# Softmax sums as 32x32 matmul tiles in one stretch per step, in a two-layer lookup convolution

## The chip, the cores and the metric

The kernel runs on one core of a Trainium2 chip. The metric is the device time in microseconds, from the first to the last instruction of one execution. The core has a matrix engine (PE, with the loading of its stationary operand listed as PEld), a vector engine (DVE), a scalar engine (ACT), GpSimd (POOL) and a sync engine (SP) that issues most of the DMAs. Each engine works through its own instructions in program order and waits on semaphores for the others.

## The reference

The input x is 16 images of 256 channels of 28x28, in float32. Each image is normalized by groups of 8 channels, sent through the block below, and added to x.

```python
def amm_conv3x3(x, centroids, w_sub):            # centroids: C=256, k=16, s=9
    p = ...                                      # 3x3 patches of each channel: B, N=784, C, 9
    d = sum(p * p) - 2.0 * einsum('bncs,cks->bnck', p, centroids) + sum(centroids ** 2)
    attn = softmax(-d, axis=-1)                  # over the 16 codes of each channel
    lut = einsum('cks,cso->cko', centroids, w_sub)
    return einsum('bnck,cko->bno', attn, lut)

out = relu(bn1(amm_conv3x3(gn(x), centroids1, wsub1)))
out = bn2(amm_conv3x3(out, centroids2, wsub2))
out = out * sigmoid(relu(mean(out) @ w1 + b1) @ w2 + b2)
result = x + relu(out + gn(x))
```

So for each pixel and each channel there are 16 logits, one from each code, a softmax over the 16, and a sum over 256 channels and 16 codes into 256 outputs. This is done twice.

## The kernel before

The kernel never forms the table `lut`. Where the exponentials e of a channel's 16 logits are there, the nine taps of its softmax-weighted code are nine numerators (e times the codes) over one denominator (the sum of e). The numerators over the denominator, times `w_sub`, summed over channels and taps, are the output.

**Blocks and steps.** The work is cut into 128 blocks. A block is one layer, one image, one half of the 784 pixels (392 of them) and one half of the 256 channels. Each image and layer has four blocks (`BLOCKS`), and the kernel goes through them in order. A block takes two steps, so that there are some 256 steps in all. What is done in a step belongs to several blocks at once: the logits of one, the sums of the one before, the products of blocks before that.

**The order.** Nothing is scheduled by a tool. `at(step, place, function, ...)` puts a call into a table, the table is sorted by step and place, and the calls are made in that order. Every engine gets its instructions in this order and runs them as a queue.

**The matmuls of a step**, all in float32, each recorded as two passes over the array:

- `logits` (line 613, tile `lg`): patches times codes. One call is 16 matmuls of 32 rows by 32 columns, one for each of the 16 sub-arrays that the 128x128 array can be split into. There are four calls (mm = 0 to 3) for each block, two in a step. `exps` (line 624, ACT) reads each result out of PSUM and writes e, 820 ns for a half of it.
- `num_b` (line 678, tile `nb`): the denominators and the ninth numerator of a block. It is 32 matmuls of 64 rows by 32 columns, so that eight sub-arrays are used at once, in every second step.
- `num_a` (line 664, tile `na`): the other eight numerators, 32 matmuls of 64 rows by 32 columns, in the steps between.
- `product` (line 748, tile `acc`): numerators over denominators times weights, 128x128, up to nine matmuls in a step and 63 in eight steps. The 63 come from a scheme that saves products with sums and differences of the four blocks (`PRODUCTS`); the differences are made by `mix` on POOL (lines 755 and 757).

The order on PE in a step is `lg`, then `na` or `nb`, then `lg`, then `acc`.

**From sums to quotients.** `split_r` (line 688, ACT) and `join_r` (line 692, DVE) take the denominators out of `nb`, `recip_dve` (line 706) inverts them, `spread` (line 721) copies them to the rows of the numerators, and each numerator is then either scaled by DVE straight out of PSUM (`scale_a`, line 740) or copied by ACT (`copy_a`, line 734) and scaled by POOL (`scale_q`, line 729). The results lie in the tiles `qp` (pairs) and `qo` (ones), from which `product` reads.

**PSUM** is four buffers of two banks each. Every matmul result above takes one of them, by a fixed table (`ROLES`, and `EARLY` for the first steps).

In layer 2 and the first half of the channels (`wide`), one of the four e tiles of a block is not exponentiated at once, but copied, turned, reduced by its maximum and exponentiated later (`wide_copy` to `wide_exp`).

Of the kernel before, what the change touches and what calls it, by code (L numbers as in the profile page):

```python
# [8 lines left out]
F32 = mybir.dt.float32  # L9
# [8 lines left out]
P = 128  # L18
# [21 lines left out]
NQ = {"pair": 12, "one": 4}  # L40
KO = (2, 3, 4, 5, 6, 7, 8, 0, 1)
SLOT_MM = (1, 0, 2, 3)
BLOCKS = ((0, 0), (0, 1), (1, 1), (1, 0))
# [18 lines left out]
ORDER = (4, 0, 1, 2, 3)  # L62
QUEUE = (None, None, (-0.9, 0.0), (-0.4, 0.0), (0, 1.5), (1, 1.5), (4, 0.35), (5, 1.5))
# [19 lines left out]
def rows_of(m, c, a):  # L83
    r, c4, mm = c >> 1, 2 * (c & 1) + a, m & 3
    return r, c4, mm, 16 * r + 4 * mm + c4, 16 * (1 - r) + 4 * mm + c4
# [3 lines left out]
def kernel(  # L89
# [83 lines left out]
    epool = ctx.enter_context(tc.tile_pool(name="epool", bufs=7))  # L173
# [116 lines left out]
    m_cw = kst[:, 3:7]  # L290
# [42 lines left out]
    def small_bank(name, step, tag=None):  # L333
        return bank(name, step, step and ROLES["small"][step % 2], EARLY["small"].get(step) if tag is None else tag)
# [323 lines left out]
    def num_a(u, mm):  # L658
        slot, tags = SLOT_MM.index(mm), fixed(u, "na")
        bs = banks("na", after(u, 2), ROLES["na"][slot], tags and tags[slot])  # L660
        es = u["e", mm]
        for i in range(4):
            for r in range(2):
                nc.tensor.matmul(  # L664
                    bs[32 * i : 32 * i + 32, r, :N],
                    lhsT=wts["cwa", u["hh"]][64 * r : 64 * r + 64, mm, i, :],
                    rhs=es[64 * r : 64 * r + 64, i, :],
                    start=True, stop=True,
                )
        u["na", mm] = bs  # L670
# [37 lines left out]
    def mask_of(k):  # L708
        if k == 8:
            return [(xx + 16) % 32 for xx in range(32)]  # L710
        mm, r = divmod(k, 2)
        return [16 * (1 - r) + 4 * mm + (xx >> 3) for xx in range(32)]
# [22 lines left out]

    def scale_a(u, mm):
# [7 lines left out]
    def product(key, us, w, ks, first=True, last=True, step=None, cols=(0, N), tag=None):  # L744
        if first and key not in accs:
            accs[key] = bank("acc", step, step and ROLES["acc"][step % 2], EARLY["acc"].get(step) if tag is None else tag)
# [105 lines left out]
    def rank_score(o):  # L852
        nc.vector.tensor_reduce(score[:, o : o + 1], hpads[o], axis=AX.X, op=ALU.max)
        nc.vector.tensor_scalar_mul(score[:, o : o + 1], score[:, o : o + 1], posn[:, o : o + 1])
        wide = small.tile([P, 32], F32, name="score_w")
# [130 lines left out]
    def prep_cwa():  # L986
# [3 lines left out]
        for c in range(4):  # L990
            nc.vector.tensor_scalar(f[:, :, 8 * c : 8 * c + 8], src[:, :, 0:8], m_cw[:, c : c + 1], None, op0=ALU.mult)
# [234 lines left out]

    def wide_next(j):
# [8 lines left out]
    for j, u in enumerate(blocks):  # L1236
        gi, g = 8 * (j // 4), 2 * j
        for mm in range(5):
            kind = "one" if mm == 4 else "pair"
            t = g + 1 + (j > 2) if mm == 4 else g + 2 + (j > 1)  # L1240
            homes.append(((t, 1.0), 1, j, mm, kind))
            homes.append(((gi + LAST[u["r"]][0], LAST[u["r"]][1] + 0.01 * ORDER[mm]), 0, j, mm, kind))
# [6 lines left out]

    for j, u in enumerate(blocks):  # L1250
        g = 2 * j
        u["w"] = j
        wide = u["l"] == 1 and u["hh"] == 0
        for p in range(2):
# [6 lines left out]
            for q in range(2):  # L1261
                mm = 2 * p + q
                cl, sub = TURN.get((j, mm), (g + p, 0.1 + (0.2 * q if j < 3 else q)))
                at(cl, sub, logits, u, mm)
                if wide and mm == 0:
                    at(g, 0.12, wide_copy, u, mm)
                    at(g, 0.9, wide_turn, u, mm)
                    at(g, 1.38, wide_max, u, mm)
                    at(g, 1.39, wide_sub, u, mm)
                    at(g + 1, 1.22, wide_back, u, mm)  # L1270
                    at(g + 1, 1.89, wide_exp, u, mm)
                else:
                    at(cl, 1.06 if (cl, sub) == (4, 1.035) else sub + 0.01, exps, u, mm)
# [8 lines left out]
        g = 2 * j + 2 + (j > 1)  # L1282
        for i, mm in enumerate(SLOT_MM):
            at(g, 1.0 + 0.01 * i, num_a, u, mm)
# [440 lines left out]
```

## Time and profile before

| | |
|---|---|
| time, median of 2 runs | 2605.55 us (2605.37 to 2605.73) |
| the profiled execution, first to last instruction | 2606.2 us |
| mean granted clock of PE | 0.999 |
| busy share PE / DVE / ACT / POOL | 99% / 68% / 53% / 73% |

The profile is of one execution. A busy time is the time in which an engine has at least one instruction under way, so that a PE with one sub-array at work is as busy as one with sixteen. The mean duration of one matmul pass (some 0.5 us) is from its start until its result has landed; passes overlap, and what a group costs is read from when the next group starts. The tile of a matmul, such as 64*32, gives rows by columns of the array that it takes.

### The profile page before, as it was taken

How to read it: one execution, taken by the hardware profiler on the slowest of the kernel's cores; microseconds unless marked ns; L12 is line 12 of the kernel's file. 1: busy time of each engine (PE TensorE's matmuls, PEld its weight loads, DVE VectorE, ACT ScalarE, POOL GpSimd, SP SyncE). 2: the span in 40 equal slices, each digit the busy share in tenths (PEclk: the TensorE clock that was granted, in tenths of full speed). 3: DMA queues.
4: the chain of work that ended last, by engine and by line, in shares of the span. 5: the costliest groups of instructions: out<-in, count | busy, mean ns of one | idle time of the engine just before them, and what ended most of it. 6: DMA issues, size and time to landing. Idle time of an engine off the chain costs nothing.

```text
span 2606.2 us, 85832 instructions
## 1 busy us (share of the span) xinstructions
PE 2591.2 (99%) x37026; PEld 1273.2 (49%) x37026; DVE 1776.6 (68%) x3797; ACT 1371.7 (53%) x1913; POOL 1905.6 (73%) x1341
## 2 busy tenths in 40 slices
PE   8999999999999999999999999999999999999999
PEld 4444455444454444544444444444444444444445
DVE  8766656666657666566676767766776667767676
ACT  6444444444444445444445555555555655555565
POOL 6687666776567776667666887878878787787786
PEclk9999999999999999999999999999999999999999
DMA  7556656565545575564664444444344444444442
GB/s 228 166 131 184 195 166 187 160 168 170 163 141 147 157 194 173 165 172 134 176 169 103 109 112 127 119 119 120 101 126 128 118 116 112 115 124 128 117 104 66
DMA packets 213288, 372.07 MB, mean 143 GB/s; under 512 B 29496, under 2 KB 183528, under 8 KB 212328
## 3 DMA queue, kind: packets, MB, share of 16 engines
q1 hardware_dynamic: 206584, 333.75, 47.6%
q0 software_dynamic: 6176, 32.66, 3.5%
q8 instruction: 295, 4.83, 0.8%
q14 instruction: 89, 0.73, 0.1%
q10 hardware_dynamic: 144, 0.10, 0.0%
HBM read 288.46 MB, written 77.95 MB: 141 GB/s over the span
## 4 chain that ended last, share of the span: by engine, by line
PE 99%; ACT 0%; POOL 0%; DVE 0%; issue 0%; DMA 0%; POOLq 0%; ACTq 0%
PE acc L748 52%; PE lg L613 17%; PE na L664 14%; PE nb L678 14%; ACT e L624 0%; PE sep L1049 0%; POOL qp L757 0%; PE sep L1041 0%; DMA xt<-in_x 0%; PE tap L392 0%; PE sqp L374 0%; PE sqp L343 0%; POOL qp L729 0%; PE gnp L534 0%; PE gnp L551 0%
## 5 line engine op out<-in xcount | busy, mean ns | idle before, releaser
L748 PE MATMUL acc<-qp,wall 128*128 128x392 f32 (+1 forms) x3088 | 1097.5, 498 | 0.3 <-POOL qp L757 0.2
L624 ACT ACTIVATE e<-lg 128x784 f32<-128x784 f32 x960 | 737.8, 820 | 635.2 <-PE lg L613 632.0
L757 POOL TENSOR_TENSOR qp<-qp,qp 128x784 f32<-128x784 f32 x512 | 943.7, 1867 | 152.0 <-DVE qp L740 151.6
L748 PEld LDWEIGHTS acc<-qp,wall 128*128 128x128 f32 x3088 | 567.4, 190 | 504.8 <-issue 53.6
L721 DVE STREAM_SHUFFLE rb<-r 128x392 f32<-128x392 f32 x1024 | 551.5, 606 | 0.0
L613 PE MATMUL lg<-pt,wd 32*32 32x392 f32 x15872 | 469.0, 499 | 0.2
L692 DVE SCALAR_TENSOR_TENSOR r<-nb,kst,r 128x392 f32<-128x392 f32 x128 | 80.1, 626 | 447.6 <-ACT r L688 447.6
L664 PE MATMUL na<-e,cwa 64*32 64x392 f32 x8192 | 376.5, 493 | 0.0
L740 DVE TENSOR_TENSOR qp<-na,rb 128x784 f32<-128x784 f32 x352 | 334.0, 972 | 62.2 <-PE na L664 50.3
L678 PE MATMUL nb<-e,cwb 64*32 64x392 f32 x8192 | 375.2, 492 | 0.1
L729 POOL TENSOR_TENSOR qo<-qo,rb 128x392 f32<-128x392 f32 x128 | 132.5, 1035 | 297.0 <-DVE rb L717 296.2
L706 DVE RECIPROCAL r<-r 128x392 f32<-128x392 f32 x128 | 333.2, 2603 | 4.4
L729 POOL TENSOR_TENSOR qp<-qp,rb 128x784 f32<-128x784 f32 x160 | 295.7, 1858 | 2.9
L678 PEld LDWEIGHTS nb<-e,cwb 64*32 64x32 f32 x8192 | 191.5, 106 | 174.7 <-issue 24.5
L664 PEld LDWEIGHTS na<-e,cwa 64*32 64x32 f32 x8192 | 183.8, 106 | 184.0 <-issue 74.8
L613 PEld LDWEIGHTS lg<-pt,wd 32*32 32x32 f32 x15872 | 116.4, 103 | 266.6 <-issue 238.3
L748 PE MATMUL acc<-qp,w_A 128*128 128x392 f32 x512 | 182.4, 499 | 0.0
L688 ACT ACTIVATE r<-nb,kst 128x392 f32<-128x392 f32 x128 | 86.7, 678 | 165.5 <-PE nb L678 162.3
L648 POOL TENSOR_TENSOR z<-z,mx 128x1568 f32<-128x1568 f32 x32 | 91.8, 2869 | 94.8 <-DVE mx L642 94.8
L748 PE MATMUL acc<-qo,wall 128*128 128x392 f32 (+1 forms) x386 | 157.9, 491 | 0.0
L734 ACT COPY qp<-na 128x784 f32<-128x784 f32 x160 | 130.0, 813 | 23.6 <-PE na L664 22.1
L748 PEld LDWEIGHTS acc<-qp,w_A 128*128 128x128 f32 x512 | 94.6, 190 | 82.5 <-DVE qp L740 19.8
(241 smaller groups left out, 1706.4 us busy)
## 6 DMA issues: line engine op xcount, KB each, us to landing
pt<-home SPq DMA_DIRECT2D x744, 209.0 KB
pt<-home SPq DMA_DIRECT2D x744, 104.5 KB
home<-xpad SPq DMA_DIRECT2D x30, 899.0 KB
xt<-in_x SPq DMA_DIRECT2D x30, 784.0 KB
out_dram<-y SPq DMA_DIRECT2D x31, 392.0 KB
pt<-in_p SPq DMA_DIRECT2D x6, 784.0 KB
d_wS<-st SPq DMA_DIRECT2D x12, 192.0 KB
wall<-d_wS SPq DMA_DIRECT2D x4, 576.0 KB
```

What stands on the lines that cost most here:

```text
L613: nc.tensor.matmul(bk[32 * c : 32 * c + 32, :N].rearrange("p (r w) -> p r w", w=W), lhsT=(wx[u["hh"]] if early(u) else wts["wd", u["hh"]]) ...
L624: nc.scalar.activation(eg[:, 2 * i : 2 * i + 2, :], bk[:, :, :N], AF.Exp, scale=2.0)
L648: nc.gpsimd.tensor_tensor(zk, zk, mx.unsqueeze(2).to_broadcast([P, N // 4, K]), ALU.subtract)
L664: nc.tensor.matmul(bs[32 * i : 32 * i + 32, r, :N], lhsT=wts["cwa", u["hh"]][64 * r : 64 * r + 64, mm, i, :], rhs=es[64 * r : 64 * r + 64, ...
L678: nc.tensor.matmul(bs[32 * i : 32 * i + 32, r, :N], lhsT=wts["cwb", u["hh"]][64 * r : 64 * r + 64, mm, i, :], rhs=es[64 * r : 64 * r + 64, ...
L706: nc.vector.reciprocal(u["r"], u["r"])
L721: nc.vector.stream_shuffle(rb[:, r, :], u["r"], mask_of(2 * mm + r))
L729: nc.gpsimd.tensor_tensor(q, q, u.pop(("rb", mm)), ALU.mult)
L734: nc.scalar.copy(pair(u, mm), u.pop(("na", mm))[:, :, :N])
L740: nc.vector.tensor_mul(pair(u, mm), u.pop(("na", mm))[:, :, :N], rb)
L748: nc.tensor.matmul(accs[key][:, : cols[1] - cols[0]], lhsT=wl[w][:, k, :], rhs=us["q", k][:, cols[0] : cols[1]], start=first and n == 0, s ...
L757: nc.gpsimd.tensor_tensor(pair(out_u, mm), pair(in0, mm), pair(in1, mm), ALU.subtract)
```

## The change

Three things are changed together.

- `num_a` and `num_b` are cut into matmuls of 32x32 like `logits`. For the same sums this takes twice as many matmuls, each on half the rows: 64 for `na` and 64 for `nb` in place of 32 and 32.
- In the steps 10 to 251 the matmuls of `lg`, `na` and `nb` stand in one stretch (`stage_of`), and the products behind it. The stretch has six slots. A slot is two units of eight matmuls, the one on row tiles 0 and 2, the other on row tiles 1 and 3 (the two lanes). Together a slot takes all 16 sub-arrays. One lane does a logits unit, four units of denominators and a logits unit (`SUM_LANE`, "anmopb"), the other two units of numerators, two of logits, two of numerators (`TAP_LANE`, "xyabzw"). The lanes are swapped from step to step. PSUM buffers come from `LANE_TAGS`.
- For all images but the first and the last, what works on the products of an image comes a step later (`later`, `late`); products, mixes and scales are put into new orders (`KO_LANE`, `MIX_LANE`, `ORDER_LANE`). There are 14 tiles `qp` in place of 12, and 8 of e in place of 7. Two of the four numerator tiles of a block are scaled by DVE from PSUM and two are copied and scaled by POOL; one of the copies moves to DVE (`copy_dve`) outside the wide blocks. Weights and row positions are laid out to fit (`rows_of`, `mask_of`, `prep_cwa`).

```diff
+LANE_STEPS = range(10, 252)
+LANE_TAGS = (
+    {"aS": 1, "x": 2, "n": 0, "aT": 3, "bT": 1, "z": 2, "bS": 3, "acc": 1},
+    {"aS": 3, "x": 2, "n": 0, "aT": 1, "bT": 3, "z": 2, "bS": 1, "acc": 3},
+)
+SUM_LANE, TAP_LANE = "anmopb", "xyabzw"
+SUM_ORDER = (1, 2, 3, 0)
...
-    def num_a(u, mm):
...
-        for i in range(4):
-            for r in range(2):
+    def num_a(u, m2):
+        tags = fixed(u, "na")
+        for slot in (2 * m2, 2 * m2 + 1):
+            u["na", SLOT_MM[slot]] = banks("na", after(u, 2), ROLES["na"][slot], tags and tags[slot])
+        for h in range(2):
+            for lane in range(2):
+                lane_na(u, 2 * m2 + lane, h)
+
+    def lane_na(u, x, h):
+        mm, lane = 2 * (x >> 1) + h, x & 1
+        for row in (lane, lane + 2):
+            for i in range(4):
                 nc.tensor.matmul(
-                    bs[32 * i : 32 * i + 32, r, :N],
-                    lhsT=wts["cwa", u["hh"]][64 * r : 64 * r + 64, mm, i, :],
-                    rhs=es[64 * r : 64 * r + 64, i, :],
+                    u["na", x][32 * i : 32 * i + 32, row >> 1, :N],
+                    lhsT=wts["cwa", u["hh"]][32 * row : 32 * row + 32, mm, i, :],
+                    rhs=u["e", mm][32 * row : 32 * row + 32, i, :],
+                    start=(h == 0), stop=(h == 1),
+                )
+
+    def lane_nb(u, mm, lane, first, last):
+        for row in (lane, lane + 2):
+            for i in range(4):
+                nc.tensor.matmul(
+                    u["nb"][32 * i : 32 * i + 32, row >> 1, :N],
+                    lhsT=wts["cwb", u["hh"]][32 * row : 32 * row + 32, mm, i, :],
+                    rhs=u["e", mm][32 * row : 32 * row + 32, i, :],
+                    start=first, stop=last,
+                )
+
+    def lane_lg(u, mm, lane, tag):
+        t = banks("lg", tag=tag)
+        for i in (lane, lane + 2):
+            for c in range(4):
+                nc.tensor.matmul(
+                    t[32 * c : 32 * c + 32, i >> 1, :N].rearrange("p (r w) -> p r w", w=W),
+                    lhsT=wts["wd", u["hh"]][32 * i : 32 * i + 32, mm, c, :],
...
+    def lane_exp(u, mm, lane):
+        if ("e", mm) not in u:
+            u["e", mm] = epool.tile([P, 4, N], F32, tag="e", name="e")
+        dst, src = u["e", mm][:, lane::2, :], u.pop(("lg", mm, lane))[:, :, :N]
+        if is_wide(u) and mm == 0:
+            nc.scalar.copy(dst, src)
+        else:
+            nc.scalar.activation(dst, src, AF.Exp, scale=2.0)
+
+    def stage_of(s):
+        p, odd = divmod(s, 2)
+        tags = LANE_TAGS[odd]
+        lg = blocks[p]
+        nb = blocks[p - 1] if p - 1 in LANE_SUMS else None
+        na = blocks[p - 2 + odd] if p - 2 + odd in LANE_SUMS else None
...
+        def slot(k):
+            unit(SUM_LANE[k], odd, "S")
+            unit(TAP_LANE[k], 1 - odd, "T")
+
+        slot(0)
+        slot(1)
+        lane_exp(lg, mms[0], odd)
+        slot(2)
+        if na:
+            (scale_a if not odd else copy_a if wide else copy_dve)(na, taps)
+        slot(3)
+        lane_exp(lg, mms[0], 1 - odd)
...
+        slot(4)
+        lane_exp(lg, mms[1], 1 - odd)
+        slot(5)
+        if odd and nb:
+            split_r(nb)
+        lane_exp(lg, mms[1], odd)
+        if na:
+            (copy_a if odd else scale_a)(na, taps + 2)
...
+    def later(n):
+        return int(0 < n < 2 * B - 1)
...
+    for step in LANE_STEPS:
+        at(step, 0.2, stage_of, step)
...
+            late = later(n)
             for c, w, r, ks in PRODUCTS:
+                if late:
+                    ks = KO_LANE if len(ks) == NS else KO_LANE[:7] if c == 6 else KO_LANE[7:]
...
-                    at(g + c, 1.32 if g + c == 7 else 2.0, product, (n, c), us[r], w, ks, step=g + c)
+                    at(g + c + late, 1.32 if g + c == 7 else 2.0, product, (n, c), us[r], w, ks, step=g + c + late)
```

261 lines of the change are left out of this document (178 added, 83 removed).

## The prediction

> **What bounds the kernel now.** I read the page's busy shares first, then its chain of work that ended last, then the groups by line, and then the order of time on PE.
>
> ```profile
> PE 2591.2 (99%) x37026; PEld 1273.2 (49%) x37026; DVE 1776.6 (68%) x3797; ACT 1371.7 (53%) x1913; POOL 1905.6 (73%) x1341
> PE 99%; ACT 0%; POOL 0%; DVE 0%; issue 0%; DMA 0%; POOLq 0%; ACTq 0%
> ```
>
> The chain lies on PE from end to end, so a microsecond on PE is a microsecond of the span, and the other engines matter only if they become late. A busy PE says nothing of how full its sub-arrays are. For that, this is one step in order of time on PE (start, length, engine, group, count of passes), and its loads of weights in the same stretch:
>
> ```profile
> 1009.65 0.94 PE L613 MATMUL lg<-pt,wd 32*32 32x392 f32 x32
> 1010.52 2.92 PE L664 MATMUL na<-e,cwa 64*32 64x392 f32 x64
> 1013.38 0.94 PE L613 MATMUL lg<-pt,wd 32*32 32x392 f32 x32
> 1014.25 4.22 PE L748 MATMUL acc<-qp,w_A 128*128 128x392 f32 x12
> 1018.30 0.82 PE L748 MATMUL acc<-qo,w_A 128*128 128x392 f32 x2
> 1018.96 1.48 PE L748 MATMUL acc<-qp,w_A 128*128 128x392 f32 x4
> 1020.37 0.94 PE L613 MATMUL lg<-pt,wd 32*32 32x392 f32 x32
> 1021.24 2.92 PE L678 MATMUL nb<-e,cwb 64*32 64x392 f32 x64
> 1024.09 0.94 PE L613 MATMUL lg<-pt,wd 32*32 32x392 f32 x32
> ```
>
> What a group costs is the distance to the next group's start: `lg` 0.87 us, `na` 2.86 us, `lg` 0.87 us, `acc` 6.12 us. The part that the change rebuilds is 1014.25 - 1009.65 = 4.60 us of each step; the step with `nb` has the same. A pass of 128x128 takes (1018.96 - 1018.30) / 2 = 0.33 us; the same 392 columns go through a small tile in a pass. Two passes make a matmul, so a sub-array needs 0.66 us for one. By that, `lg` (16 matmuls on 16 sub-arrays, two passes deep) loses 0.87 - 0.66 = 0.21 us at its edges, `na` (eight passes deep, 2.64 us) 0.22 us, and `acc` (18 passes, 5.94 us) 0.18 us. Each change of tile shape costs some 0.2 us, four times a step.
>
> **The change part by part: the new stretch.** The change removes two of these four edges. The work itself stays equal: `na` or `nb` was 32 matmuls on 8 sub-arrays, it is now 64 on 16, half of each in every step. A step's stretch is six sets of 16 matmuls, 96 in place of 64. If a set costs 0.66 us and one edge 0.21 us, the stretch takes 6 x 0.66 + 0.21 = 4.17 us, 0.43 us less than now.
>
> But does a second set on the same 16 sub-arrays follow the first at 0.66 us? In the steady state of before it never has to: each `lg` set stands alone. At the start two stand together:
>
> ```profile
> 68.36 0.95 PE L613 MATMUL lg<-pt,first 32*32 32x392 f32 x32
> 69.04 1.29 PE L613 MATMUL lg<-pt,wd 32*32 32x392 f32 x32
> 70.29 0.52 PE L678 MATMUL nb<-e,cwb 64*32 64x392 f32 x2
> ```
>
> Two sets take 70.29 - 68.36 = 1.93 us, more than the 1.74 us of two that stand apart, edges included. The second costs 1.93 - 0.87 = 1.06 us. Why is told by the loads of another such pair that begins at 24.30, first counted in a window (window, its length, PEld busy and count; then clock and DMA), then in order of time; the last two rows count PE's passes under way in two windows:
>
> ```profile
> 24.29:24.60 0.31, 0.23 (x32) 1.00 1.50 402
> ...
> 24.66 0.10 PEld L613 LDWEIGHTS lg<-wall,first 32*32 32x32 f32 x1
> 24.99 0.10 PEld L613 LDWEIGHTS lg<-wall,first 32*32 32x32 f32 x1 [0.23 <-issue]
> 25.18 0.23 PEld L613 LDWEIGHTS lg<-wall,first 32*32 32x32 f32 x14
> ...
> 24.64:24.66 0.02, 0.02 (x16) 1.00 2.58 538
> 24.66:24.98 0.32, 0.32 (x32) 1.00 0.65 140
> ```
>
> All 32 loads of the first set go at once. At 24.66 the count of passes goes from 16 to 32: the second passes begin. The 33rd load, the first of the next set, goes in the same moment, the 34th at 24.99, and then nothing until 25.18, though the other 15 sub-arrays were as far as the first and could take weights as early. On `na`, with eight sub-arrays, the loads of the next round go out evenly, eight in each 0.33 us:
>
> ```profile
> 1010.86:1011.19 0.33, 0.21 (x8) 1.00 1.07 384
> 1011.19:1011.52 0.33, 0.21 (x8) 1.00 1.04 373
> ```
>
> In program order a matmul is four items: load, pass, load, pass. The load that is held until 25.18 is the 35th, item 69. What lies 64 items ahead of it is item 5, and item 4 is the second pass of the first matmul. It began at 24.66 and, with a mean duration of a pass on this tile of 499 ns (the row below), it has landed just before 25.18, which is 0.52 us after its start.
>
> ```profile
> L613 PE MATMUL lg<-pt,wd 32*32 32x392 f32 x15872 | 469.0, 499 | 0.2
> ```
>
> So I read it as a window of 64 items that empties in order, an item leaving when its result has landed. `na` has 32 items to a round, and the window holds two rounds; a set on 16 sub-arrays has 64, and fills it alone. [...]
>
> With such a window a matmul holds its four places for 0.33 us (first pass) + 0.52 us (second pass until landed) = 0.85 us, and 16 matmuls are all that fit. A steady set of 16 costs about 0.85 us, not 0.66. The stretch is then 0.87 (first set with its edge) + 1.06 (second, measured) + 4 x 0.85 = 5.33 us, against 4.60 now: 0.73 us more in each of the 242 steps from 10 to 251, 177 us. Bounds for the third to sixth set, which no row of before shows: 0.66 us each from below (0.87 + 1.06 + 2.64 = 4.57 us, 7 us less in all), 1.06 us each from above (6.17 us, 380 us more). I take 0.85 because it follows from the two durations that also explain the second set, whose extra is mostly the delay of the first held load.
>
> **The other steps.** In the seven blocks outside the lane steps, `na` is now four sets in a row: 0.87 + 1.06 + 2 x 0.85 = 3.63 us against 2.86, 7 x 0.77 = 5 us more. `nb` stays as it was there.
>
> **The other engines.** The step would be 5.33 + 6.12 = 11.4 us long, and their work hardly changes:
>
> ```profile
> L624 ACT ACTIVATE e<-lg 128x784 f32<-128x784 f32 x960 | 737.8, 820 | 635.2 <-PE lg L613 632.0
> L721 DVE STREAM_SHUFFLE rb<-r 128x392 f32<-128x392 f32 x1024 | 551.5, 606 | 0.0
> L740 DVE TENSOR_TENSOR qp<-na,rb 128x784 f32<-128x784 f32 x352 | 334.0, 972 | 62.2 <-PE na L664 50.3
> L706 DVE RECIPROCAL r<-r 128x392 f32<-128x392 f32 x128 | 333.2, 2603 | 4.4
> L729 POOL TENSOR_TENSOR qp<-qp,rb 128x784 f32<-128x784 f32 x160 | 295.7, 1858 | 2.9
> L692 DVE SCALAR_TENSOR_TENSOR r<-nb,kst,r 128x392 f32<-128x392 f32 x128 | 80.1, 626 | 447.6 <-ACT r L688 447.6
> ```
>
> POOL scales two numerator tiles in each block instead of 1.25, some 90 more: 90 x 1.86 = 167 us, 2073 us of the predicted span, 74%. DVE has two scales and one copy in place of 2.75 scales, ACT the same copies. So no engine becomes the bound by its sum. Free by cover, with what it costs without:
>
> - The buffer of the first `lg` unit (slot 1 of six) is written again in the fourth slot, that of the third slot in the sixth. Between lies more than 1.7 us of matmuls, against one exponential of 0.82 us on an ACT half idle. Cost if late: what is left of 0.82 us.
> - The numerators of slots 1 and 2 must be taken out by DVE before slot 5 writes there: 0.97 us within two slots of 0.85 us, if DVE is free. Cost if late: up to 0.97 us a step.
> - `nb` must be emptied before the next even step's second slot. Behind it stand 0.63 (join), 2.60 (reciprocal), 1.21 (two shuffles) and 0.63 us (join) on DVE, 5.1 us after `split_r`; a full `acc` of 6.12 us and a slot cover it. The small matmuls of normalization and gate now share that buffer and come behind odd steps' products, so that they, and all of PE's queue behind them, wait for the same join; where the product has 7 matmuls, the cover is 4.8 + 0.85 us. Cost if late: about 1 us at some 60 places, 60 us as a bound, below nothing not, since these matmuls only gain a wait. I take nothing.
> - Products a step later, with two more `qp` and one more e, ease the waits on `mix`. The whole chain waits for POOL under 0.5% of the span now, so this can gain 13 us at most; I take nothing. No transfer is moved against its consumer by more than the step that the consumer moves too.
>
> Sum: 2606.2 + 177 + 5 = 2788 us; the median of the runs is 0.7 us under the profiled span, which leaves 2788.
>
> **The rivals.**
>
> *No such window: the faster side.* If the hold at 25.18 is an accident of the start-up code and the sets follow at 0.66 us, the stretch is 4.17 us: -0.43 x 242 = -104, nothing for the early blocks, about 2501 us. The edges of 0.2 us speak for it, two real ones are removed; the measured 1.06 us speaks against it. It decides once the five later sets cost under 0.75 us each (0.87 + 5 x 0.75 = 4.6). [...]
>
> *A hold that happens once in a stretch.* If the delay is paid by the second set alone, the stretch is 4.57 us, the early blocks cost 3 us in place of 5, and the time is 2606 - 7 + 3 - 1 = 2601 us. For it: in the pair at 24.30 the loads after 25.18 run without another stop. Against: they fill the window again.
>
> *The window, and DVE late in the stretch.* If slot 5 waits for the numerators, say 0.3 us a step, 73 us come on top, 2861 us. Against: DVE has slack in a longer step.
>
> *Not what it says.* The recorded order of the new program has the units of eight alternating as described, so this has no chance of its own.
>
> **How the numbers follow.** Window 0.66, window and DVE 0.08, once 0.10, none 0.16. The predicted time is that of the first. Its own range is 2690 (a set at 0.75 us) to 2850 (at 0.9 us, with some of the 60 us). To leave out no more than 2 in 10 the range must reach the rival at 2601: 2598 to 2850 us. A difference under 2%, 52 us, is called no change: slower than 2658 has 0.66 + 0.08 = 0.74, faster than 2553 has 0.16, between them 0.10.
>
> **What would show it.** In the profile after, the stretch of a step from the first `lg` to `acc` is 5.3 us, and PEld has, in a window of 0.33 us in its middle, some 12 loads, where sets at 0.66 us would have 16. PE stays at 99% in the chain, `acc` at 6.12 us. If the stretch is 4.2 us, there is no window; if it is about 4.6 us, the hold comes once. If PE has idle times released by DVE or ACT within the stretch, the covers above were wrong.

## The result, and the profile after

| | before | after |
|---|---|---|
| time, median of 2 runs | 2605.55 us (2605.37 to 2605.73) | 2985.94 us (2979.47 to 2992.42) |
| ratio of the times | | 1.146, 95% interval 1.1401 to 1.1519 |
| the profiled execution, first to last instruction | 2606.2 us | 2990.9 us |
| mean granted clock of PE | 0.999 | 0.991 |

The kernel is slower by 380 us, 385 us between the profiled executions. The forecast was slower, at 2788 us; the size is off by 198 us, and the time lies above the range.

From the page after, its busy shares, the shares of the chain that ended last, and the group of the logits (count, busy time and mean ns of one pass, idle time of PE ahead of it and what ended most of that):

```profile
PE 2872.8 (96%) x52962; PEld 1632.9 (55%) x52962; DVE 1799.7 (60%) x3802; ACT 1395.9 (47%) x1913; POOL 2070.9 (69%) x1430
PE 81%; DVE 8%; POOL 7%; DMA 1%; issue 1%; ACT 1%; SPq 1%; DVEq 0%; POOLq 0%; ACTq 0%
L705 PE MATMUL lg<-pt,wd 32*32 32x392 f32 x15488 | 1020.7, 506 | 55.4 <-DVE half_sum L893 46.7
```

PE had 99% of the chain before and has 81% now. DVE and POOL, which had nothing of it, hold 15%. POOL's busy time is 2071 us, where 2073 were worked out: what the engines have to do was counted rightly, and none of them is full. They are late at certain places. The prediction's own sign for this, idle times of PE released by DVE within the stretch, is there: the covers were wrong.

**A step without a wait.** This is one in layer 2 in order of time on PE (start, length of the group, group, count of passes); between the rows shown lie those of the other lane:

```profile
2436.38 0.56 PE L705 MATMUL lg<-pt,wd 32*32 32x392 f32 x8
...
2437.06 0.80 PE L694 MATMUL nb<-e,cwb 32*32 32x392 f32 x8
...
2437.93 0.79 PE L694 MATMUL nb<-e,cwb 32*32 32x392 f32 x8
...
2438.74 0.84 PE L694 MATMUL nb<-e,cwb 32*32 32x392 f32 x8
...
2439.59 0.84 PE L694 MATMUL nb<-e,cwb 32*32 32x392 f32 x8
...
2440.45 0.84 PE L705 MATMUL lg<-pt,wd 32*32 32x392 f32 x8
...
2441.68 5.53 PE L856 MATMUL acc<-qp,wall 128*128 128x392 f32 x16
```

The stretch is 2441.68 - 2436.38 = 5.30 us, where 5.33 were forecast. The slots start 0.87, 0.81, 0.85 and 0.86 us apart, each of them a set of 16 matmuls, where the array kept full would have two passes of 0.33 us, 0.66 us by the forecast's estimate. The loads say the same (window, its length, PEld busy and count, clock, DMA share, GB/s):

```profile
2438.74:2439.59 0.85, 0.66 (x34) 1.00 0.00 0
2439.59:2440.45 0.86, 0.66 (x34) 1.00 0.00 0
```

These are 32 loads and two cut by the edges in 0.85 us, 12 to 13 in 0.33 us in the mean, where an array kept full would have 16. The forecast had them in each window of 0.33 us; in fact they go out in bursts, and two such windows one after the other hold 27 and 4:

```profile
2438.26:2438.59 0.33, 0.28 (x27) 1.00 0.23 50
2438.59:2438.92 0.33, 0.24 (x4) 1.00 0.00 0
```

**Where the rest went.** For each step I take from the trace the time from the stretch's first matmul to the first of the product. The 245 stretches of 192 passes have a median of 5.38 us, 135 of them are under 5.4, and their mean is 5.96. So 0.63 x 245 = 154 us lie above the forecast stretch. The products, from their first matmul to the next stretch, take 1446 us in all, 51 more than before (1395). With the 182 us that were forecast this is 387, against the 385 measured. The waits of PE in the page after (engine, line, waited for: us in total, times, longest) name two places:

```profile
PE lg L705 <- DVE half_sum L893: 46.7, 29, 3.3
PE acc L856 <- POOL qp L865: 24.0, 17, 1.5
```

**The first place** is the step behind the product of two taps (four passes), once in each image and layer. In layer 1:

```profile
542.70 0.93 PE L856 MATMUL acc<-qp,wall 128*128 128x392 f32 x2
...
544.21 0.56 PE L705 MATMUL lg<-pt,wd 32*32 32x392 f32 x8
...
545.77 1.11 PE L694 MATMUL nb<-e,cwb 32*32 32x392 f32 x15
549.11 0.91 PE L705 MATMUL lg<-pt,wd 32*32 32x392 f32 x8 [2.23 <-DVE half_sum L893]
...
554.02 5.53 PE L856 MATMUL acc<-qp,wall 128*128 128x392 f32 x16
```

DVE in the same time:

```profile
542.80 0.97 DVE L846 TENSOR_TENSOR qp<-na,rb 128x784 f32<-128x784 f32 x1 [1.41 <-PE na L684]
543.70 1.02 DVE L438 BATCH_NORM_STATS2 gn_st<-xt 128x6 f32<-128x392 f32 x2
...
546.03 0.60 DVE L822 STREAM_SHUFFLE rb<-r 128x392 f32<-128x392 f32 x1
...
548.50 0.56 DVE L893 TENSOR_TENSOR half_sum<-acc,half_sum 128x392 f32<-128x392 f32 x1
```

The third slot's logits unit is to write PSUM buffer 1, which the product of the step before holds (`LANE_TAGS`: `aT` of an odd step and `acc` of an even one). It is free when DVE has added that product to `half_sum`. In DVE's queue this addition stands behind the scaling, the group statistics of the next image (2.3 us) and five shuffles (2.5 us). The product ended at 544.2; it is taken out at 548.5. The stretch takes 554.02 - 544.21 = 9.81 us. Such stretches have a median of 9.84 us in layer 1 (14 of them, 58 us above 5.33 in sum) and 7.45 us in layer 2 (16, 31 us).

**The second place** is the product of 18 passes behind that stretch, in layer 2. On PE, then on POOL:

```profile
2404.57 4.22 PE L856 MATMUL acc<-qp,wall 128*128 128x392 f32 x12
2410.24 1.58 PE L856 MATMUL acc<-qp,wall 128*128 128x392 f32 x4 [1.46 <-POOL qp L865]
2412.30 0.93 PE L856 MATMUL acc<-qo,wall 128*128 128x392 f32 x2 [0.48 <-POOL qo L863]
```

```profile
2399.83 2.87 POOL L662 TENSOR_TENSOR z<-z,mx 128x1568 f32<-128x1568 f32 x1
2402.66 1.87 POOL L830 TENSOR_TENSOR qp<-qp,rb 128x784 f32<-128x784 f32 x1
...
2411.24 1.01 POOL L863 TENSOR_TENSOR qo<-qo,qo 128x392 f32<-128x392 f32 x1
```

POOL works without a pause from 2397.99 on. Ahead of that it stood idle for 4.93 and 2.85 us, waiting for tiles that DVE scales, so that its late start is in part DVE's. The mixes that the product reads stand in its queue behind the subtraction of the wide block's maxima, and PE takes each of them when it ends. The product takes 8.90 us (median of 16) in place of 6.12, 44 us in sum.

**The clock.** Two windows in the stall above (busy times by engine, then the granted clock, DMA share, GB/s):

```profile
549.00:550.00 1.00, 0.89 (x32) 0.46 (x33) 0.94 (x2) 0.00 (x0) 0.92 (x2) 0.53 1.13 183
551.00:552.00 1.00, 1.00 (x34) 0.46 (x13) 0.00 (x0) 0.60 (x1) 1.00 (x1) 0.50 0.13 49
```

Around the end of the idle time PE goes to half its clock, 0.53 and 0.50 in these windows. There are 14 such periods ahead of the kernel's end, 55 us together, ten of them in these stalls and the other four right behind idle times of 1.7 to 2.4 us that no semaphore ends; before had one, in its start-up. Twelve of the 14 last 3.41 us, the other two 6.83. Of the stalled stretches of layer 1 three run at the full clock and take 8.36 us, with the same idle time of 2.23 us; those with a period of 3.4 us at half clock take 9.7 to 9.9, with idle times of 2.23 to 2.35 us. So the idle time alone does not decide it here; what does, no run takes apart.

### The profile page after: what moved, and what is told of

Its sections match the earlier page's. It is cut to its first block, busy times and chain, and to the rows that moved or that the text cites. A ratio compares the mean times of both kernels' runs of the same rounds, so it can differ in the third digit from the quotient of the medians.

```text
span 2990.9 us, 117542 instructions
## 1 busy us (share of the span) xinstructions
PE 2872.8 (96%) x52962; PEld 1632.9 (55%) x52962; DVE 1799.7 (60%) x3802; ACT 1395.9 (47%) x1913; POOL 2070.9 (69%) x1430
## 4 chain that ended last, share of the span: by engine, by line
PE 81%; DVE 8%; POOL 7%; DMA 1%; issue 1%; ACT 1%; SPq 1%; DVEq 0%; POOLq 0%; ACTq 0%
PE acc L856 39%; PE nb L694 17%; PE lg L705 15%; PE na L684 9%; POOL qp L865 3%; DVE rb L822 2%; POOL z L662 2%; DVE qp L846 1%; DMA pt<-home 1%; POOL qp L830 1%; DVE e L666 1%; DVE gn_st L438 1%; DVE z L649 1%; PE lg L627 1%; POOL qo L863 1%
## 5 line engine op out<-in xcount | busy, mean ns | idle before, releaser
L705 PE MATMUL lg<-pt,wd 32*32 32x392 f32 x15488 | 1020.7, 506 | 55.4 <-DVE half_sum L893 46.7
L684 PE MATMUL na<-e,cwa 32*32 32x392 f32 x16384 | 959.2, 501 | 7.1 <-issue 5.3
L694 PE MATMUL nb<-e,cwb 32*32 32x392 f32 x15488 | 912.5, 503 | 3.9 <-DVE gn_dv L556 2.4
L694 PEld LDWEIGHTS nb<-e,cwb 32*32 32x32 f32 x15488 | 481.2, 103 | 248.3 <-issue 52.7
L830 POOL TENSOR_TENSOR qp<-qp,rb 128x784 f32<-128x784 f32 x249 | 460.2, 1856 | 169.8 <-DVE rb L822 169.5
L846 DVE TENSOR_TENSOR qp<-na,rb 128x784 f32<-128x784 f32 x263 | 255.6, 974 | 363.0 <-PE na L684 358.5
L705 PEld LDWEIGHTS lg<-pt,wd 32*32 32x32 f32 x15488 | 307.0, 103 | 257.1 <-issue 137.2
L684 PEld LDWEIGHTS na<-e,cwa 32*32 32x32 f32 x16384 | 288.9, 103 | 74.5 <-issue 33.1
L840 DVE COPY qp<-na 128x784 f32<-128x784 f32 x89 | 86.7, 975 | 195.9 <-PE na L684 195.9
L928 POOL DMA_INDIRECT home<-hpad,col x60 | 60.2, 1004 | 207.2 <-ACT hpad L907 125.5
```

Of the source, the lines that this page charges most:

```text
L684: nc.tensor.matmul(u["na", x][32 * i : 32 * i + 32, row >> 1, :N], lhsT=wts["cwa", u["hh"]][32 * row : 32 * row + 32, mm, i, :], rhs=u["e" ...
L694: nc.tensor.matmul(u["nb"][32 * i : 32 * i + 32, row >> 1, :N], lhsT=wts["cwb", u["hh"]][32 * row : 32 * row + 32, mm, i, :], rhs=u["e", m ...
L705: nc.tensor.matmul(t[32 * c : 32 * c + 32, i >> 1, :N].rearrange("p (r w) -> p r w", w=W), lhsT=wts["wd", u["hh"]][32 * i : 32 * i + 32, m ...
L830: nc.gpsimd.tensor_tensor(q, q, u.pop(("rb", mm)), ALU.mult)
L840: nc.vector.tensor_copy(pair(u, mm), u.pop(("na", mm))[:, :, :N])
L846: nc.vector.tensor_mul(pair(u, mm), u.pop(("na", mm))[:, :, :N], rb)
```

## The experiments

The times are medians of two runs, those of runs 1 to 4 single ones, beside the kernel before on the same chip (2605 to 2607 us in every case). Two runs of one version differ by up to 15 us, so a smaller difference between two versions says nothing by itself. In the table are the medians, in us, of the stretch behind the shorter part of the split product (14 places in layer 1, 16 in layer 2), and of the product of 18 passes behind it, by layer.

| kernel | time | stretch, layer 1 | stretch, layer 2 | product, layer 1 | product, layer 2 |
|---|---|---|---|---|---|
| the change | 2985.9 | 9.84 | 7.45 | 6.24 | 8.90 |
| taps 5 and 4 (1) | 2945.0 | 7.10 | 5.91 | 6.24 | 8.87 |
| small matmuls' buffer (2) | 3002.0 | 9.11 | 7.52 | 6.24 | 8.89 |
| both of these (3) | 2950.9 | 7.10 | 6.22 | 6.24 | 8.87 |
| addition first (6) | 2999.4 | 8.26 | 6.05 | 7.93 | 10.64 |
| and subtraction on DVE (7) | 3004.0 | 8.60 | 6.06 | 7.91 | 11.00 |
| addition first, statistics later (8) | 2963.0 | 5.97 | 6.09 | 6.53 | 10.63 |
| no subtraction (9) | 2956.4 | 9.82 | 7.44 | 6.24 | 6.97 |
| taps 5 and 4, statistics later (10) | 2948.0 | 5.34 | 6.13 | 6.24 | 8.87 |
| and subtraction on DVE (12) | 2930.4 | 5.33 | 7.86 | 6.24 | 6.57 |

**1. The split product, five taps and four.**

```diff
-ks = KO_LANE if len(ks) == NS else KO_LANE[:7] if c == 6 else KO_LANE[7:]
+ks = KO_LANE if len(ks) == NS else KO_LANE[:5] if c == 6 else KO_LANE[5:]
```

> The changed kernel with the products S1 of an image split 5 and 4 taps over its two steps in place of 7 and 2 (images 2 to 31). Theory A (the step whose product has 2 taps is too short for DVE, which must add the accumulator to half_sum before the third slot of the next stretch can use its buffer): the stretch behind that step falls from a mean of 8.2 us to below 6 us, and the time by 60 to 90 us, to about 2910. Rival B (the long stretches come from the clock or from POOL's late qp tiles, whatever the split): the same steps stay long, the time within 15 us of 2986.

2944.99 us, 41 less, where 60 to 90 were expected. The waits of PE in its profile:

```profile
PE lg L705 <- DVE half_sum L893: 13.1, 13, 2.0
PE sep L1155 <- DVE qo L804: 18.1, 14, 1.3
```

The wait for `half_sum` falls from 46.7 to 13.1 us: the longer the product, the more of DVE's queue it covers. A part comes back as a new wait, since the gate's small matmuls in layer 2 now stand behind a product of five taps where they had seven, and their buffer is not yet empty.

**2. The small matmuls in another PSUM buffer** than `nb`.

```diff
-tag = LANE_TAGS[1]["n"] if step in LANE_STEPS else EARLY["small"].get(step)
+tag = LANE_TAGS[1]["x"] if step in LANE_STEPS else EARLY["small"].get(step)
```

> The changed kernel with the small matmuls of normalization and gate on the buffer of the numerators instead of the buffer of the denominators, in the lane steps. Theory A (these matmuls wait on PE for the join of the denominators, and all of PE behind them): the product groups with two small matmuls in layer 2 fall from 8.9 to about 6.4 us, 15 times, 35 to 50 us in all, to about 2945. Rival B (they wait for something else, such as their inputs): the groups stay at 8.9 us and the time at 2986.

3002.02 us, no gain. The long products stay at 8.9 us. They don't wait for the small matmuls ahead of them.

**3. Both edits.**

> Both edits together. Theory A: the two waits lie at different places and add up, 2986 - 75 - 40 = about 2870; the stretch stays at 5.31 to 5.33 us in undisturbed steps, so that 2606 + 177 + 5 = 2788 is not passed. Rival B (one stall only hides the other, PE catches up on neither): no more than the better of the two alone.

2950.87 us, no better than the first edit alone, where 2870 were expected. The new wait of run 1 is gone with the other buffer (18.1 us; the five-tap products of layer 2, with the gate's matmuls behind them, fall by 21), but stretches in other steps are 30 us longer in sum. So the shared buffer costs nothing in the change and 18 us where the product ahead of it is shorter.

**4. The kernel before, with only `num_a` recut** to matmuls of 32x32. The order `lg`, `na`, `lg`, `acc` stays, `nb` stays at 64x32, and no product moves.

```diff
...
-lhsT=wts["cwa", u["hh"]][64 * r : 64 * r + 64, mm, i, :],
-rhs=es[64 * r : 64 * r + 64, i, :],
+lhsT=wts["cwa", u["hh"]][32 * row : 32 * row + 32, mm, i, :],
+rhs=u["e", mm][32 * row : 32 * row + 32, i, :],
...
```

> The kernel before with the numerators alone cut to 32x32 (with the layout of weights that they need); denominators stay 64x32, the order stays lg, na, lg, acc, and nothing is moved to another step. The stretch lg, na, lg is then six sets of 16 matmuls of one tile shape, in every second step. Theory A (a window of 64 items, emptied in order as results land): 5.3 us for it in place of 4.6, 0.73 x 128 = 93 us more, about 2700. Rival B (no window; the 5.3 us of the changed kernel are waits on ACT and DVE inside its slots): the two edges saved show, 4.2 us, about 2551.

2763.97 us. A step in order of time on PE:

```profile
712.47 0.94 PE L613 MATMUL lg<-pt,wd 32*32 32x392 f32 x32
713.26 3.58 PE L670 MATMUL na<-e,cwa 32*32 32x392 f32 x119
...
717.92 1.25 PE L753 MATMUL acc<-qp,wall 128*128 128x392 f32 x3
```

The stretch takes 717.92 - 712.47 = 5.45 us. The 124 stretches that hold `na` have a median of 5.54 us and the 124 with the `nb` of before one of 4.59. So the smaller tiles alone, with nothing moved and two edges fewer, cost 0.95 us a step, more than the 0.73 forecast. The whole is 158 us longer, where 93 were expected: 0.95 x 124 = 118 us are this, and of the rest 21 are idle times of PE without a semaphore, which run 5 comes back to.

**5. The window by itself.** The kernel before, where only the logits unit is recut: each of its 16 matmuls becomes two of 196 columns, 16 first halves and then 16 second halves. The columns streamed stay the same, the items are 128 in place of 64.

```diff
+for h in range(2):
     for i in range(4):
...
-rhs=side(u, mm // 2, 4 * (mm % 2) + c)[32 * i : 32 * i + 32],
+rhs=side(u, mm // 2, 4 * (mm % 2) + c)[32 * i : 32 * i + 32, RT // 2 * h : RT // 2 * h + RT // 2],
...
```

> The kernel before, with only its logits unit recut: each of the 16 matmuls of 392 columns becomes two of 196, all first halves before all second halves; the other units, the order of the steps and every wait stay. Same columns streamed, twice as many items. Theory A (the window of 64 items, emptied in order as results land): 32 matmuls with their loads are 128 items, twice the window, so the second half is held for the landing of the first: a logits unit 0.87 -> about 1.2 us, two in a step and 248 steps, +0.3 to 0.4 us a unit: 2605 + about 178 = 2785 us (2730 to 2800). Theory B (no window; matmuls of 32x32 tiles simply run side by side and the 0.85 us of a set come from the columns or from a fixed price of a set): a unit stays at 0.87 to 0.95 us, 2605 to 2640 us. Theory C (each matmul instruction has a fixed price of its own beyond its columns): also slower, but then the units of one set, too, would show passes further apart than 6 to 7 ns where they start.

2830.48 us, ratio 1.086 (1.083 to 1.089), above the 2730 to 2800 us expected. One step, and the counts (PE, then PEld) in windows of the unit that starts at 1106.02:

```profile
1106.02 1.29 PE L614 MATMUL lg<-pt,wd 32*32 32x196 f32 x64
1107.24 2.86 PE L679 MATMUL nb<-e,cwb 64*32 64x392 f32 x64
```

```profile
1106.01:1106.13 0.12, 0.12 (x17) 0.11 (x29) 0.01 (x1) 0.00 (x0) 0.00 (x0) 1.00 0.17 56
1106.02:1106.35 0.33, 0.33 (x33) 0.29 (x33) 0.23 (x2) 0.00 (x0) 0.00 (x0) 1.00 0.17 46
1106.35:1106.68 0.33, 0.33 (x41) 0.22 (x15) 0.33 (x1) 0.00 (x0) 0.23 (x1) 1.00 0.11 20
```

A unit takes 1.22 us (the median of 499 as well) in place of 0.87, as theory A expected. 33 loads go out in the first 0.33 us, the next at 0.38, and then none until 0.54 us after the start. That is when the second pass of the first matmul lands: it began at 0.19 us, and a pass of 196 columns lasts 0.33 us in the mean. (The ends of passes are modelled in the profile, so "landed" is its reading.) Theory C falls, since 17 passes begin within 0.12 us. Theory B falls. Of the 224 us, 0.35 x 499 = 175 are the longer units by their median; the mean unit takes 1.30 us. In the remainder lie waits on `lg` that no semaphore explains, 28 us in sum, and eight periods at half clock; what else is in it I have not followed.

Such idle times of PE have a common sign in the traces of all versions. The page counts the transfers of instructions (queue, kind: transfers, MB, share of the 16 DMA engines); here before, in the change and in run 5:

```profile
q8 instruction: 295, 4.83, 0.8%
q8 instruction: 419, 6.86, 1.0%
q8 instruction: 423, 6.93, 1.1%
```

PE has 31,872 passes and loads more in the change than before, which is 257 for each of the 124 transfers more. Past the start-up the kernel before has no idle time of PE over 0.6 us that no semaphore ends. The other versions' traces have 140 of them, and each ends 1.2 to 1.8 us after such a transfer has landed; of the 457 that a semaphore ends, 14 do. So I read them as waits of PE for its own instructions, of which the kernels with more and smaller matmuls transfer more (419 and 423 times here, in place of 295): 12 us in the change, 21 in run 4, 23 in run 5, 24 in run 11. No run takes this apart.

**6. The addition to `half_sum` first,** right behind the scaling and ahead of the statistics and the shuffles.

```diff
-at(g + c + late, 1.32 if g + c == 7 else 2.0, product, (n, c), us[r], w, ks, step=g + c + late)
+at(g + c + late, 1.32 if g + c == 7 else 1.0 if late and c == 7 else 2.0, product, (n, c), us[r], w, ks, step=g + c + late)
...
-at(*((e + 8, 0.0) if n else (7, 1.36)), acc_add, l, b, None, (n, 7))
+at(*((e + 7, 1.05) if late else (e + 8, 0.0) if n else (7, 1.36)), acc_add, l, b, None, (n, 7))
...
-at(*(((g + 1, 1.5) if b == 1 else (g, 0.3)) if b else (4, 0.14)), gn_stats, b + 1, q)
+at(*(((g + 1, 1.5) if b == 1 else (g, 1.06)) if b else (4, 0.14)), gn_stats, b + 1, q)
```

> The changed kernel with VectorE's order changed in one place of a step: in images 2 and later the addition that takes the two-tap product's accumulator to half_sum stands right behind the scaling of the step's tiles, ahead of the group statistics of the next image (layer 1) and of the five shuffles; nothing is left out. Theory A (the stall behind the two-tap product is VectorE's order: buffer 1 of the accumulators is handed on late): the stretch behind that product falls from 8.22 us in the mean to 5.3 to 5.8, 75 to 92 us go, and most of the half-clock windows go with the idle time: 2895 to 2915 us. Theory B (VectorE has too much to do there in whatever order; what is put behind the addition is then late itself): the wait moves to the shuffles' users, the scalings on GpSimd and the product behind them, and the time falls by less than 40 us: 2945 us or more.

2999.37 us, no gain. The waits of PE:

```profile
PE acc L856 <- POOL qp L865: 44.3, 30, 2.1
PE na L684 <- DVE qp L840: 28.5, 13, 3.2
```

The wait for `half_sum` is gone and two others are there. DVE's copy of the next numerators is late in layer 1. The shuffles are late for POOL, and the product behind, in both layers (7.93 and 10.64 us). The stretches behind the short product give back 31 us in sum, and the products behind them take 52 more. That is theory B: an order can't mend it, because a step with a product of 1.5 us lasts some 6.8 us and has more than that for DVE to do (scaling 1.0 us, addition 0.6, statistics 2.3, shuffles 2.5, copy 1.0, and behind these the join and the reciprocal of 2.6).

**7. And the subtraction of the maxima on DVE.**

```diff
-nc.gpsimd.tensor_tensor(zk, zk, mx.unsqueeze(2).to_broadcast([P, N // 4, K]), ALU.subtract)
+nc.vector.tensor_tensor(zk, zk, mx.unsqueeze(2).to_broadcast([P, N // 4, K]), ALU.subtract)
```

> The kernel of the run before this (the addition to half_sum ahead of the shuffles) and with it the subtraction of the maxima of the wide blocks (128x1568) on VectorE instead of GpSimd; nothing is left out. Theory A (the product of 18 taps in the second layer, 8.9 us instead of 6.3, waits for GpSimd's operands because GpSimd has 2.86 us of that subtraction in the same step): these 15 groups fall to 6.3 to 6.8 us, 30 to 38 us go beyond the run before: 2860 to 2880 us. Theory B (GpSimd is late there by more than that subtraction, or VectorE, which takes some 1.7 us more in that step, is late in its place): less than 15 us go, or the time rises.

3003.98 us, no gain. The product in layer 2 stays late: its median is 11.00 us in place of 10.64, and the 16 products lie 72 us above 6.12 in sum, where it was 74. POOL is relieved, but DVE, already late there, gets the work. That is theory B; that it is DVE on which the products now wait is argued from run 6 and not shown apart.

**8. The statistics a step later,** with the addition first: in layer 1 they leave the short step for the long one behind it.

```diff
-at(*(((g + 1, 1.5) if b == 1 else (g, 1.06)) if b else (4, 0.14)), gn_stats, b + 1, q)
+at(*(((g + 1, 1.5) if b == 1 else (g + 1, 0.3)) if b else (4, 0.14)), gn_stats, b + 1, q)
```

> The kernel that has the addition to half_sum ahead of the shuffles, and with it the group statistics of the next image (layer 1, 2.4 us of VectorE) moved out of the step with the two-tap product into the step after it, which has a product of 18 matmuls; nothing is left out. Theory A (the step with the two-tap product lasts 6.8 us of TensorE and holds more VectorE work than that, in whatever order; GpSimd and the next product inherit the lateness): in layer 1 the excess behind the two-tap product falls from 49 to 20 us or less and the excess of the product after it from 26 to 5 us or less, layer 2, which has no such statistics, stays; the time falls by 45 to 60 us, to 2935 to 2955 us. Theory B (what is late there is not VectorE's amount of work but the landing of a transfer or GpSimd): less than 15 us go.

2962.99 us, 36 less than the run it builds on. In layer 1 the stretch goes from 8.26 to 5.97 us and the product from 7.93 to 6.53, 51 us in sum. Layer 2, which has no such statistics, stays at 6.09 and 10.63. So it is the amount of DVE's work in that step, as theory A says. The time fell by less than the 45 us expected, because the stretches of steps 8n + 4 and 8n + 5 in layer 1 rise by 16 us.

**9. The subtraction left out,** in the change itself.

```diff
-at(g, 2.52, wide_sub, u, 0)
...
-nc.scalar.activation(eg, eg, AF.Exp, scale=2.0)
+nc.scalar.activation(eg, eg, AF.Exp, scale=0.001)
```

> The changed kernel with the subtraction of the maxima of the wide blocks left out (GpSimd, 2.86 us, 32 times); the exponential behind it is given a small scale so that its numbers stay finite. VectorE's work and order stay. Theory A (the product of 18 taps in the second layer, 8.9 us instead of 6.3, is late because GpSimd has too much in that step): its excess of 38 us falls below 10 us, and the time to 2945 to 2960 us. Theory B (GpSimd's operands come late from VectorE, and GpSimd's amount doesn't matter): the excess stays above 25 us, 2970 us or more.

2956.43 us, 30 less. The product in layer 2 takes 6.97 us in place of 8.90, and of PE's wait for the mixes, 24.0 us before, this is left:

```profile
PE acc L856 <- POOL qp L865: 0.5, 1, 0.5
```

DVE's order was the same, so POOL's amount in that step is the cause of 31 of the 44 us: the products in layer 2 are still 13 us above 6.12 in sum, and what part of those comes from DVE's late tiles no run takes apart.

**10. Taps 5 and 4, and the statistics later.** The edits of 1 and 8, without the addition first.

> The changed kernel with two mends at once: the nine taps of the split product cut 5 and 4 instead of 7 and 2, which gave 2945 us alone, and the group statistics of layer 1 moved out of the step with the shorter half into the step after it; the addition to half_sum stays where the change has it. Nothing is left out. Theory A (too much VectorE work in a short step): the 27 us of excess left in layer 1 behind the shorter half fall to 5 to 10, layer 2 stays, 2915 to 2930 us. Theory B (the rest is something else): 2940 us or more. In either case the time stays above 2788 us, since the six sets of 16 matmuls of a stretch stay at 5.3 us.

2948.01 us (2945 to 2951), no gain on the 2944.99 of run 1, where 2915 to 2930 were expected. The stretch in layer 1 is mended, 5.34 us in place of 7.10, 18 us in sum. The gain is lost at two other places: the stretches of steps 8n + 5 in layer 1, which were at 5.34 us in run 1, are back at 6.45 (12 us), and those of the short step itself rise (5 us).

**11. A transfer a step later.** Those stretches of step 8n + 5 show a third loss. In the change all 15 of layer 1 take 6.1 to 8.5 us, 19 us above 5.33 in sum; the 42 us that the expectation names were counted wrongly.

```diff
-at(*((g + 4, 1.92) if b else (4 + 4 * q, 1.6 - 0.05 * q)), to_home1, b + 1, q)
+at(*((g + 5, 1.92) if b else (4 + 4 * q, 1.6 - 0.05 * q)), to_home1, b + 1, q)
```

> The changed kernel with one transfer of layer 1 issued a step later: the next image's padded rows to its home in DRAM (899 KB), which in the changed kernel lie over the stretch of step 8n + 5, the one that takes 6.4 us instead of 5.3 with no semaphore waited for (42 us in all). Nothing is left out, no other order is changed. Theory A (that transfer disturbs TensorE's loads while it runs): the 1.1 us leave that stretch, and come up in the stretch of step 8n + 6 or go: the excess at the old place falls below 15 us. Theory B (the excess has to do with that place in the program and not with the transfer): it stays at 30 to 45 us. The time of the whole, 2986 us, moves by less than 30 us either way.

2989.05 us. Windows over one such stretch in the change, in run 11, over the stretch behind it in run 11, and over the same stretch in run 1 (the last three numbers are clock, DMA share and GB/s):

```profile
689.61:696.04 6.43, 6.43 (x194) 3.55 (x193) 1.66 (x3) 3.80 (x6) 2.59 (x3) 1.00 0.90 317
```

```profile
697.61:702.96 5.35, 5.35 (x194) 3.50 (x193) 1.67 (x3) 3.71 (x6) 2.61 (x3) 1.00 0.25 93
709.08:714.39 5.31, 5.31 (x194) 3.33 (x193) 2.57 (x6) 2.50 (x4) 0.00 (x0) 1.00 0.92 338
```

```profile
671.85:677.19 5.34, 5.34 (x193) 3.48 (x192) 1.66 (x3) 3.69 (x6) 2.60 (x3) 1.00 0.97 367
```

With the transfer gone from it the stretch falls to 5.35 us (median of 15; 1.5 us above the forecast in sum). So the transfer has a part in it. It is not enough by itself: over the next stretch it does no harm in this image, while in others that stretch takes 6.5 to 9.6 us, with PE idle and no semaphore waited for, the idle times of run 5 (17.5 us in sum for layer 1); and in run 1 it lies over the old stretch at full bandwidth, which takes 5.34 us. What else has to come together is open.

**12. Run 10, with the subtraction on DVE.**

> The kernel with the nine taps cut 5 and 4 and the group statistics a step later (2948 us), and with it the subtraction of the maxima of the wide blocks on VectorE instead of GpSimd, since leaving it out took 29 us from the product of 18 taps in the second layer. Nothing is left out. Theory A (with a longer short step VectorE has room for it, and GpSimd is relieved of 2.86 us): that product's excess falls from 38 us to below 15, 2915 to 2930 us. Theory B (VectorE is as full there as GpSimd, so that the work can't be placed on either): the excess stays above 25 us or comes up in the stretch, 2940 us or more.

2930.43 us, ratio 1.125 (1.118 to 1.132), the fastest of the versions and still 326 us behind the kernel before. The product in layer 2 is mended (6.57 us, 34 us in sum), but the stretch ahead of it rises from 6.13 to 7.86 (35 us): what POOL no longer has to do is now late on DVE, as theory B expected. The profiled execution is 22 us shorter than that of run 10 all the same, and some 17 of these lie in layer 1, which has no wide blocks and so nothing that this edit changes; the largest part, 11 us, is in the stretches of step 8n + 5. That the time came very near theory A's range is therefore luck, and no gain of the edit is shown.

## Why the prediction was wrong in its size

**What held.** The window, counted in the forecast as 64 items from the loads of before, was the largest step of the sum, and its times were right: 5.30 us for a stretch without a wait (5.33 forecast), slots 0.85 us apart, and run 5, where the same work in twice as many items takes 1.22 us in place of 0.87, its loads held once 34 of 64 are out. The hold and its times are measured; that it counts 64 items, and keeps a place until the result has landed, is a reading of these rows. The rivals without a window and with one hold in a stretch fall by the same rows. Run 4 has the sign with no other part of the change, at 0.95 us a step in place of 0.73. `acc` stayed at 6.12 us in steps without a wait, and POOL's sum was right to 2 us. That small matmuls share a buffer with `nb` was rightly taken at nothing in the change: run 2 moves them, and gains nothing. With the product of five taps ahead of them (run 1) it costs 18 us.

**What failed** is the part of the sum on free cover: "their work hardly changes", "no engine becomes the bound by its sum", and the list of what is covered.

- The list held the buffers of the logits units among themselves, of the numerators and of `nb`. It left out that a logits unit also takes over the accumulator of the step before, and so waits for DVE to take that product out. For 30 stretches this costs 89 us, part of it half clock. The waits at the place are read from the profile, and runs 1, 6 and 8 show the cause: not the order in DVE's queue but the amount of its work in a step whose product is only two taps long. A step was treated as 11.4 us long throughout; this one has 1.5 + 5.3 us. A cover has to be taken at the shortest step.
- "Products a step later ... I take nothing" was the other. In layer 2 one product of 18 passes is late by 2.8 us behind POOL, 44 us in all. POOL at 74% of the span said nothing of that step, in which it works without a pause for over ten microseconds. Run 9 takes the subtraction away, and 31 of the 44 us go with it.
- The half clock (14 periods, 55 us together) was no term at all. It comes with the idle times above, and most of it lies inside the 89 us.
- The stretches of step 8n + 5 (19 us) were not foreseen. A transfer has a part in them; the rest is open, and so are some 50 us of small excesses in other steps, which no run takes apart. The idle times that look like waits for instructions are 12 of these 50; the sum had no term for them either.

So 182 us are the forecast mechanism, 89 and 44 the two covers that failed, 19 the third place, which leaves some 50. The rival "window, and DVE late in the stretch" came nearest with 2861 us. It had DVE late by a little in every step, in the numerators, while the stalls sit in one step of eight, at another buffer, and are large.

No version here beats the kernel before, and none could while the stretch stays as it is: with every wait mended the forecast's sum of 2788 us would be left. That is argued from rows; no run reached it.

## What to carry to other kernels

In the change a set of 16 matmuls on sixteen sub-arrays, of two loads and two passes each, started 0.81 to 0.87 us after the one before it, where two passes of 0.33 us would be 0.66; in run 5 the loads were held once 34 were out. So count loads and passes, not sub-arrays, before a matmul on eight sub-arrays is cut in two for sixteen. When every buffer is passed on within a step, list for each buffer who frees it, on which engine, and what stands ahead of that in the engine's queue, and take the cover from the shortest step and not from the mean one. Where an engine is late by the amount of its work in one step, another order only moves the wait: lengthen that step, or move work to a longer one, and look again for the place where the gain is given back.

## What the runs showed of the hardware

- In run 5, of the 64 loads of a unit, 33 went out in the first 0.33 us and 15 in the next 0.33, one of these 0.38 us after the start and the others from 0.54 us on, when the first matmul's second pass had landed by the profile's reading. A unit of 32 matmuls with half the columns takes 1.22 us, one of 16 with all of them 0.87.
- An idle time of PE of 2.23 us was followed by a period of 3.4 us at half clock, which made an 8.36 us stretch 9.8 us long; in three stretches the same idle time was followed by none. Mending a stall can pay twice for that reason: run 10 has four such periods in its whole span, the change 15, those of the start and the end included. But run 12, the fastest version, has ten.
- A transfer at 0.90 of the DMA engines lay over a stretch that lost 1.1 us without any semaphore wait, and one at 0.97 over the same stretch of another version that lost nothing.
- Idle times of PE without a semaphore ended 1.2 to 1.8 us after a transfer of instructions had landed, 140 times out of 140. The transfers hold 16 KB each, one for some 257 passes and loads, and there are 419 in the change where there were 295.
